# Reordering VectorE, ScalarE and GpSimd work at the passage between two transformer layers and inside the last attention pair

## The chip, the cores and the metric

The kernel is one program on one core of a Trainium2 chip. The core has a matrix engine (TensorE, PE in the profile; its loads of the stationary operand are shown as PEld), three elementwise engines (VectorE or DVE, ScalarE or ACT, GpSimd or POOL) and a sync engine (SyncE or SP), which here issues nearly all DMAs. Each engine runs its own list of instructions in order; semaphores tie the lists together. The metric is the device time of one execution in microseconds (us), taken as the median of the runs.

## The reference

A graph network block over 1024 nodes with 512 features: a graph convolution, four transformer layers, a second graph convolution, and residuals. Cut to the layer loop, which is where the change lies:

```python
for i in range(L):                                     # L = 4
    a = _attn(_ln(h, ln2_w[i], ln2_b[i]), cond, Wq[i], Wk[i], Wv[i], Wo[i])
    h = h + a
    u = _ln(h, ln3_w[i], ln3_b[i]) @ geglu_w[i] + geglu_b[i]
    val, gate = jnp.split(u, 2, axis=-1)
    f = val * jax.nn.gelu(gate, approximate=False)
    h = h + f @ ffo_w[i] + ffo_b[i]
```

`_attn` is cross attention: 16 batches of 64 queries, 256 conditioning rows each, 8 heads of 64. All is float32.

## The kernel before

The residual stream `h` stays on chip as eight blocks of 128 nodes by 512 features (`hall`; `h[nb]` is one block). A layer has an attention part, which runs over eight groups g (each a block of 128 query rows with its two batches of conditioning rows), and a feed-forward part in four stretches r.

Large products are done in fewer multiplications: a product of 2 x 2 blocks is computed as seven block products of sums and differences of blocks. The sums have to be made beforehand by DVE or POOL: `weight_sums` for the query weights (tiles `wqs`, four POOL instructions), `sum_first` for the normalised rows (`ln2S`), `geglu_weights` for the feed-forward weights (`ges`), `ln3_sums` (`ln3S`). Key and value products (`Twelve`) are instead done in three terms of reduced width: `right_parts` and `left_parts` split an operand x into a high part (`bh`, `ah`, by ACT), a low part (`bl`, `al`, by DVE) and a third (`bs` by DVE, `as` by POOL). Such a product has a `begin` (two terms, then ACT scales the PSUM bank in place, L373) and an `end` (third term, then a copy out by ACT, L380, or by DVE, L378). `staggered` runs a list of them so that the end of one follows the beginning of the next, and calls the functions of `beside` behind chosen ones.

PSUM has eight banks, handed out in turn; a new tile waits until the last reader of the bank's old tile is done. `pin` keeps an instruction in program order; `in_order(engine)` ties all instructions of one engine inside the block into the order in which they are written; `waiting_for(ins, engine)` makes the engine's instructions inside wait for `ins`; `issue_after(ins)` places instructions behind `ins` on their engine. What is not tied is placed by a scheduler.

**Inside the attention (g = 6).** `scores` makes the softmax, `keys` and `values` the products for the next group, and `mix` the weighting by the probabilities: it transposes the probabilities on PE (`tr_pr`), copies them out (`pT`, two by ACT, two by DVE at L880), multiplies (`po`, L866) and copies the result (`oT`, L889). At g = 6, after `mix`, `ln3_norm(4, 5)` normalises two blocks of `h`: statistics (L168, L169), a reciprocal root by a dozen small DVE operations (`rsqrt`, L151 to L160), and a scaling (`xn`, L189). Their transposes (`ln3_turn`, `tr_ln`) come after the transposes of blocks 0 to 3 and the last value product. At the same g POOL makes the four `ges` sums.

**The passage from layer l to l + 1.** The last output half of the feed-forward, `ffn_out(l, R - 1, 1, ...)`, adds seven products out of the banks `fa` to `fd` onto `h` (L1229, L1233, L1243). Its argument `beside` holds functions for other DVE work that is placed at fixed points: the roots of the first four blocks (`ready_first`), and, right behind the first product, `split_cond` (`al_c`, L314) and the moments of the first half of the blocks (`take_moments`). Behind it come the split of the value weights (`bl_wv`, `bs_wv`), the moments and roots of the second half (`less_ln`, L1344). DVE is tied in order through all this. Then the new layer starts: keys and values of group 0 by `staggered`, and beside them the scaling of the rows by ACT (`scaled_by_act`, four `xn` each, L1350) and their transposes (`turn_first`, `tr_ln`), taken out of PSUM by ACT (L810) and DVE (L808) in turn into `ln2T`. ACT is tied in order. `sum_first` makes the row sums of blocks 0 and 4, 1 and 5 on POOL and of the others on DVE (L231 to L234), and the queries (`QueryQuad`, products `qa` to `qd`) follow.

Of the kernel before, what the change touches and what calls it, by code (L numbers as in the profile page):

```python
# [14 lines left out]
OP = mybir.AluOpType  # L15
# [5 lines left out]
TINY = 2.0 ** -12  # L21
# [4 lines left out]
def gnn_kernel(  # L26
# [26 lines left out]
    nc = tc.nc  # L53
# [247 lines left out]
    def twelve_bits(t):  # L301
        return t.bitcast(F32R)
# [17 lines left out]
    def right_parts(x, name, room=None):  # L320

        parts = [slots_of(len(x), f"{n}_{name}") for n in ("bh", "bl", "bs")]
        for i, (h, l, s, x) in enumerate(zip(*parts, x)):
            nc.scalar.mul(twelve_bits(h), x, INWARD / TINY)
            for k in range(2):
                hk, lk, sk = (t[:, k, :] for t in (h, l, s))
                nc.vector.scalar_tensor_tensor(twelve_bits(l)[:, k, :], x[:, k, :], 1.0 / TINY, hk,
                                               OP.mult, OP.subtract)
                if room:
                    more = room(f"{name}_{i}_{k}")  # L330
                    nc.scalar.mul(more, hk, TINY)
                    nc.gpsimd.tensor_tensor(twelve_bits(s)[:, k, :], lk, more, OP.subtract)
                else:
                    nc.vector.scalar_tensor_tensor(twelve_bits(s)[:, k, :], hk, -TINY, lk,
                                                   OP.mult, OP.add)
        return parts

    def split_cond(l, g):
# [64 lines left out]
    def keys(l, g, wk, n=0, by=(0, 1)):  # L403

        to = blocks_in(kTs, g, f"kT_{l}_{g}")
        return [Twelve(f"k_{l}_{g}_{c}", wk, c, conds[g], to(c), by[c % 2]) for c in range(n, KC)]
# [127 lines left out]
    for i in range(2):  # L534
        for k in range(KC):
            hk = h0T[i][k // 2][:, k % 2, :]
# [316 lines left out]
    def mix(l, g, probs, v, hooks, each=pin):  # L853

        oT = t512(f"oT_{l}_{g}")
        po = bank(f"po_{l}_{g}")

        def weigh(c2, pTs):
            for a in range(2):
                c = 2 * c2 + a  # L860
                for b in range(2):
                    for m in range(MB):
                        for j in range(2):
                            n0 = c * P + b * NPG
                            at = (a * MB + m) * P + b * NPG
                            each(nc.tensor.matmul(  # L866
                                po[j * DH:(j + 1) * DH, n0:n0 + NPG],
                                v[b][:, m, c * P + j * DH:c * P + (j + 1) * DH],
                                pTs[j][:, at:at + NPG],
                                start=(m == 0), stop=(m == MB - 1)))  # L870

        turned = []
        for c2 in range(2):
            pTs = []
            for j in range(2):
                u = 2 * c2 + j
                pt = transposed(probs[u], f"pr_{l}_{g}_{u}", each)
                pT = t512(f"pT_{l}_{g}_{u}")
                if j:
                    nc.vector.tensor_copy(pT, pt)  # L880
                else:
                    nc.scalar.copy(pT, pt)
                pTs.append(pT)
            turned.append(pTs)
            hooks[c2]()
        weigh(0, turned[0])
        hooks[2]()
        weigh(1, turned[1])
        nc.vector.tensor_copy(oT, po)  # L889
        return oT  # L890

    def attn_out(l, g, oT, wo):
# [317 lines left out]
    def ffn_out(l, r, s, left, right, kept, each=lambda ins: ins, beside=()):  # L1210

        n = f"{l}_{r}_{s}"
        u = kept[s]
        a, b, c, d = (bank(f"{x}_{n}") for x in ("fa", "fb", "fc", "fd"))
        h11, h12, h21, h22 = (hall[:, 4 * i + 2 * s:4 * i + 2 * s + 2, j * M:(j + 1) * M]
                              for i in range(2) for j in range(2))

        def product(i, to, start):  # L1220
            for q in range(2):
                for k in range(2):
                    each(nc.tensor.matmul(to[:, q * M:(q + 1) * M],  # L1223
                                          left[i][k][:, (2 * s + q) * P:(2 * s + q + 1) * P],
                                          right[i][:, k, :], start=start and q == 0 and k == 0,
                                          stop=q == 1 and k == 1, skip_group_check=True))

        def add(to, of):
            each(nc.vector.tensor_tensor(to, halves_of(of), to, OP.add))  # L1229

        product(0, a, True)
        if r:
            each(nc.vector.tensor_tensor(u, a, u, OP.add))  # L1233
            for do in beside[2:]:
                do()
        else:
            nc.scalar.copy(u, a)
        product(6, c, True)
        add(h22, c)
        product(4, d, True)  # L1240
        add(h22, d)
        product(5, b, True)
        each(nc.vector.tensor_tensor(u, b, u, OP.add))  # L1243
        if r == R - 1:
            for to in (h22, h21, h12):
                add(to, u)
        for do in beside[:1]:
            do()
        product(1, a, False)
        add(h11, a)  # L1250
        for do in beside[1:2]:
            do()
        product(3, c, False)
        add(h21, c)
        product(2, d, False)
        add(h12, d)
# [83 lines left out]
    def scaled_by_act(blocks, mv, root, name):  # L1340

        n = len(blocks)
        less = small.tile([P, 4], F32, tag="less", name=f"less_{name}", bufs=2)[:, :n]
        scaled_by_act.last = nc.vector.scalar_tensor_tensor(less, mv.rearrange("p (n c) -> p n c", c=2)[:, :, 0], -1.0,  # L1344
                                       root, OP.mult, OP.mult)

        def scale():
            for i, nb in enumerate(blocks):
                xns[nb] = t512(f"xn_{name}_{nb}")
                nc.scalar.activation(xns[nb], h[nb], AF.Identity, bias=less[:, i:i + 1],  # L1350
                                     scale=root[:, i:i + 1])

        return scale
# [54 lines left out]
    for l in range(L):  # L1408

        lnS = []  # L1410
        if l:
            units = keys(l, 0, wk, by=(0, 0)) + values(l, 0, wv, by=(0, 0))
            to_turn = [0, 1, 4, 5], [2, 3, 6, 7]
        else:
            scale_first(1, deviations(mv_first[1], "ln2_0_4"))
            with waiting_for(scale_first.last, mybir.EngineType.Pool):
                wq = weight_sums(wq, "wqs_0")
            kTs[0], vs[0], kTs[1] = (begun[n] for n in ("k0", "v0", "k1"))
            units = keys(0, 0, wk, 2) + values(0, 0, wv, 1)
            to_turn = [0, 1, 2, 3], [4, 5, 6, 7]  # L1420

        def turn_some():
            nonlocal lnT, wq
            if l:
                lnT = [slots_of(2, f"ln2T_{l}_{i}") for i in range(2)]
            turn_first(l, to_turn[0])
            lnS.extend(ln_sums(l))
            if l:
                sum_first(nc.gpsimd, 0)
                sum_first(nc.gpsimd, 1)  # L1430
                with waiting_for(scaled_by_act.last, mybir.EngineType.Pool):
                    wq = weight_sums(wq, f"wqs_{l}")

        beside = {len(units) - 1: lambda: turn_first(l, to_turn[1])}
        if l:
            beside.update({1: to_scale.pop(0), 4: turn_some, 5: to_scale.pop(0)})
            with in_order(mybir.EngineType.Activation):
                staggered(units, beside)
        else:
            staggered(units, {2: turn_some, **beside})  # L1440
# [74 lines left out]
        for g in range(NG - 1):  # L1515
# [20 lines left out]
            v = values(l, g + 1, wv)  # L1536
            oTs.append(mix(l, g, probs, vs.pop(g), (k[-1].end, nothing, v[0].begin)))
            if g == NG - 2:
                ln3_norm(g - 2, g - 1)
            if g in (1, 2):  # L1540
                base_of(2 * l + g - 1)
            if l == 0:
# [182 lines left out]
        else:  # L1725
# [6 lines left out]
                for part, t in zip(wk, right_parts(raw_wk[i:i + 1], f"wk_{l + 1}_{i}")):  # L1732
                    part.extend(t)

            def condition_and_moments():
                split_cond(l + 1, 0)
                take_moments(l + 1, half[0])

            half = [0, 1, 4, 5], [2, 3, 6, 7]
            with in_order(mybir.EngineType.DVE):  # L1740
                ffn_out(l, R - 1, 0, fT, wff, kept, pin, (lambda: split_wk(0), lambda: split_wk(1)))
                ffn_out(l, R - 1, 1, fT, wff, kept, pin, (lambda: ready_first(l + 1, half[0]),
                                                          lambda: None, condition_and_moments))
                wq = load_w(Wq[l + 1], f"wq_{l + 1}")
                ffb = load_row(ffo_b, (l + 1) * D, f"ffb_{l + 1}")
                load_cond(l + 1, 1)
                wv = right_parts(raw_wv, f"wv_{l + 1}")
                take_moments(l + 1, half[1])
                ready_first(l + 1, half[1])
# [144 lines left out]
```

## Time and profile before

| what | us |
|---|---|
| median of the runs | 2437.28 |
| lowest and highest of three runs | 2433.90, 2438.86 |
| the profiled execution | 2432.47 |
| its span, first to last instruction | 2430.6 |
| DMA busy, mean of 16 engines, main queue | 16.6% |

The profile's page comes from one execution. Busy times are sums over instructions; PE's is of pipelined matmuls, so a busy PE is not a PE at its peak. A row of a timeline has the start in us from the beginning of the span, the length, the engine, the line of the kernel, the operation, `output<-input` with shapes, the number of equal instructions merged in the row, and in brackets the idle time of the engine before it with what ended that. A row of the view of waits has who waited for whom, and then total us, times and longest. A row of the view by windows has the stretch, its length, the busy time and count of instructions of PE, PEld, DVE, ACT and POOL, then the clock granted to PE (1 is full), the share of the DMA engines, and GB/s.

### The profile page before, as it was taken

How to read it: one execution, taken by the hardware profiler on the slowest of the kernel's cores; microseconds unless marked ns; L12 is line 12 of the kernel's file. 1: busy time of each engine (PE TensorE's matmuls, PEld its weight loads, DVE VectorE, ACT ScalarE, POOL GpSimd, SP SyncE). 2: the span in 40 equal slices, each digit the busy share in tenths (PEclk: the TensorE clock that was granted, in tenths of full speed). 3: DMA queues.
4: the chain of work that ended last, by engine and by line, in shares of the span. 5: the costliest groups of instructions: out<-in, count | busy, mean ns of one | idle time of the engine just before them, and what ended most of it. 6: DMA issues, size and time to landing. Idle time of an engine off the chain costs nothing. (4 is left out here: it accounts for less than half of the span.)

```text
span 2430.6 us, 33690 instructions
## 1 busy us (share of the span) xinstructions
PE 2367.9 (97%) x12528; PEld 1776.1 (73%) x12528; DVE 1596.9 (66%) x3016; ACT 999.5 (41%) x2023; POOL 940.0 (39%) x839
## 2 busy tenths in 40 slices
PE   8999999999989999999999999999999999999999
PEld 5668886677757887577776887477775888567787
DVE  9875456787764456877775455777785445678764
ACT  7444454343344444343343444433334444434320
POOL 0142233565233223565432223455514223356531
PEclk9999999999999999999999999999999999999999
DMA  6142110111301110021201101021121111011140
GB/s 199 31 140 83 57 66 18 47 41 53 109 31 61 40 49 23 22 65 44 104 15 64 66 19 53 9 61 44 44 91 53 44 53 35 18 52 35 53 148 36
DMA packets 108843, 138.31 MB, mean 57 GB/s; under 512 B 8232, under 2 KB 65904, under 8 KB 108672
## 3 DMA queue, kind: packets, MB, share of 16 engines
q1 hardware_dynamic: 106576, 130.64, 16.6%
q0 software_dynamic: 1376, 4.30, 0.5%
q8 instruction: 104, 1.70, 0.3%
q10 hardware_dynamic: 720, 1.11, 0.1%
q14 instruction: 67, 0.55, 0.1%
HBM read 119.25 MB, written 16.78 MB: 56 GB/s over the span
## 5 line engine op out<-in xcount | busy, mean ns | idle before, releaser
L316 POOL TENSOR_TENSOR as_c<-ah_c,al_c 128x512 fp32r<-128x512 f32 x128 | 189.6, 1511 | 191.8 <-DVE al_c L314 185.8
L1122 ACT ACTIVATE g<-g 128x512 f32<-128x512 f32 x192 | 112.1, 584 | 280.0 <-PE g L1108 277.5
L373 ACT ACTIVATE v<-v 128x512 f32<-128x512 f32 x127 | 74.0, 582 | 235.0 <-PE v L362 232.8
L1059 POOL TENSOR_TENSOR gsa<-gha,gla 128x512 fp32r<-128x512 f32 x96 | 125.8, 1331 | 103.8 <-DVE gla L1056 103.8
L1059 POOL TENSOR_TENSOR gsb<-ghb,glb 128x512 fp32r<-128x512 f32 x48 | 70.1, 1460 | 219.0 <-DVE glb L1056 219.0
L362 PE MATMUL v<-bh_wv,ah_c 128*128 128x512 f32 x508 | 148.3, 414 | 0.0
L362 PE MATMUL v<-bs_wv,as_c 128*128 128x512 f32 x508 | 144.1, 405 | 2.6 <-ACT v L373 2.4
L843 ACT ACTIVATE pr<-sc,nmax 128x256 f32<-128x256 f32 x256 | 118.1, 474 | 58.4 <-DVE nmax L838 58.4
L373 ACT ACTIVATE k<-k 128x512 f32<-128x512 f32 x125 | 72.6, 585 | 164.5 <-PE k L362 164.1
L362 PE MATMUL v<-bl_wv,al_c 128*128 128x512 f32 x508 | 137.0, 392 | 0.0
L1108 PE MATMUL g<-gr,gsa 128*128 128x512 f32 x384 | 136.4, 436 | 0.0
L1135 ACT ACTIVATE g<-g,gcols 128x512 f32<-128x512 f32 x96 | 67.5, 703 | 164.8 <-DVE g L1143 161.7
L362 PE MATMUL k<-ah_c,bh_wk 128*128 128x512 f32 x500 | 135.1, 392 | 0.0
L362 PE MATMUL k<-al_c,bl_wk 128*128 128x512 f32 x500 | 134.0, 390 | 0.0
L362 PE MATMUL k<-as_c,bs_wk 128*128 128x512 f32 x500 | 132.2, 395 | 0.0
L915 POOL TENSOR_TENSOR os<-oT 128x256 f32<-128x256 f32 x12 | 8.8, 734 | 318.8 <-DVE oT L889 318.8
L1223 PE MATMUL fa<-wff,fT 128*128 128x256 f32 x512 | 121.9, 381 | 6.7 <-DVE kept L1233 6.7
L1108 PE MATMUL g<-gr,gha 128*128 128x512 f32 x384 | 122.9, 401 | 0.0
L1108 PE MATMUL g<-gl,gla 128*128 128x512 f32 x384 | 119.0, 391 | 0.0
L1223 PEld LDWEIGHTS fa<-wff,fT 128*128 128x128 f32 x512 | 96.5, 190 | 26.7 <-DVE kept L1233 9.9
L362 PEld LDWEIGHTS v<-bs_wv,as_c 128*128 128x128 f32 x508 | 93.4, 188 | 28.9 <-ACT v L373 5.2
L314 DVE SCALAR_TENSOR_TENSOR al_c<-ah_c,ct 128x1024 fp32r<-128x1024 f32 x64 | 92.2, 1445 | 33.0 <-ACT ah_c L313 33.0
(368 smaller groups left out, 5891.2 us busy)
## 6 DMA issues: line engine op xcount, KB each, us to landing
ct<-cond_dram SPq DMA_DIRECT2D x48, 512.0 KB, 4.2
wff<-in_L_gnn_ffo_w_dram SPq DMA_DIRECT2D x32, 512.0 KB, 4.3
gxb<-in_L_gnn_geglu_w_dram SPq DMA_DIRECT2D x96, 128.0 KB, 2.2
gxa<-in_L_gnn_geglu_w_dram SPq DMA_DIRECT2D x96, 128.0 KB, 2.2
cond<-in_L_gnn_cond_dram SPq DMA_DIRECT2D x32, 256.0 KB, 3.5
cond_dram<-ct SPq DMA_DIRECT2D x16, 512.0 KB, 4.1
wk<-in_L_gnn_Wk_dram SPq DMA_DIRECT2D x8, 512.0 KB, 6.3
wv<-in_L_gnn_Wv_dram SPq DMA_DIRECT2D x8, 512.0 KB, 8.4
```

The source lines that it names most:

```text
L314: nc.vector.scalar_tensor_tensor(twelve_bits(l), h, -1.0 / TINY, x, OP.mult, OP.add)
L316: nc.gpsimd.tensor_tensor(twelve_bits(s)[:, k, :], h[:, k, :], l[:, k, :], OP.subtract)
L362: pin(nc.tensor.matmul(self.bank, twelve_bits(left[k // 2])[:, k % 2, self.c * P:(self.c + 1) * P], twelve_bits(right[k // 2])[:, k % 2, : ...
L373: nc.scalar.mul(self.bank, self.bank, 1.0 + TINY)
L843: nc.scalar.activation(pr3[:, a, :], ps3[:, a, :], AF.Exp, bias=nmax[:, a:a + 1], accum_out=tot[:, a:a + 1])
L915: t.tensor_tensor(s1, a21, a22, OP.add)
L1059: pin(nc.gpsimd.tensor_tensor(s_at, h_at, l_at, OP.subtract))
L1108: pin(nc.tensor.matmul(to, self.part(i, which)[:, k, :], self.rights[i][which].bitcast(F32R)[:, k, :], start=start and k == 0, stop=stop a ...
L1122: pin(nc.scalar.mul(to, to, 1.0 + TINY))
L1135: pin(nc.scalar.activation(to, of, AF.Gelu, bias=gcols[:, cg:cg + 1]))
L1223: each(nc.tensor.matmul(to[:, q * M:(q + 1) * M], left[i][k][:, (2 * s + q) * P:(2 * s + q + 1) * P], right[i][:, k, :], start=start and q ...
```

## The change

Four edits, all of order; no instruction is added or taken away.

1. In the passage: `ffn_out` calls only `beside[2]` (the split of the conditioning rows) behind its first product, and the rest (now the moments, a function of their own) after the adds of `fc` and `fd`.
2. In the passage: the query weights' sums are made ahead of the row sums on POOL, and wait for the last instruction of the value weights' split (`right_parts.last`) instead of that of the row scaling's preparation (`scaled_by_act.last`). The key tiles are allocated ahead of them.
3. In the passage: the four row scalings by ACT are called two at a time, one product apart.
4. In every layer, g = 6: `ln3_norm(4, 5)` is placed behind the copy `oT` of `mix`.

On PE and SyncE the order of instructions is the same before and after.

```diff
@@ right_parts
-                    nc.vector.scalar_tensor_tensor(twelve_bits(s)[:, k, :], hk, -TINY, lk,
-                                                   OP.mult, OP.add)
+                    right_parts.last = nc.vector.scalar_tensor_tensor(
+                        twelve_bits(s)[:, k, :], hk, -TINY, lk, OP.mult, OP.add)
@@ mix
-        nc.vector.tensor_copy(oT, po)
+        mix.last = nc.vector.tensor_copy(oT, po)
@@ ffn_out
         if r:
             each(nc.vector.tensor_tensor(u, a, u, OP.add))
-            for do in beside[2:]:
+            for do in beside[2:3]:
                 do()
...
         add(h22, d)
+        for do in beside[3:]:
+            do()
         product(5, b, True)
@@ scaled_by_act
-        def scale():
-            for i, nb in enumerate(blocks):
+        def scale(*which):
+            for i in which or range(n):
+                nb = blocks[i]
@@ the start of a layer
             units = keys(l, 0, wk, by=(0, 0)) + values(l, 0, wv, by=(0, 0))
+            units[0].to()
+            with waiting_for(right_parts.last, mybir.EngineType.Pool):
+                wq = weight_sums(wq, f"wqs_{l}")
...
                 sum_first(nc.gpsimd, 0)
                 sum_first(nc.gpsimd, 1)
-                with waiting_for(scaled_by_act.last, mybir.EngineType.Pool):
-                    wq = weight_sums(wq, f"wqs_{l}")
...
-            beside.update({1: to_scale.pop(0), 4: turn_some, 5: to_scale.pop(0)})
+            first, then = to_scale
+            to_scale.clear()
+            beside.update({1: lambda: first(0, 1), 2: lambda: first(2, 3), 4: turn_some,
+                           5: lambda: then(0, 1), 6: lambda: then(2, 3)})
@@ attention
             if g == NG - 2:
-                ln3_norm(g - 2, g - 1)
+                ln3_norm(g - 2, g - 1, behind=mix.last)
@@ the end of a layer
-            def condition_and_moments():
-                split_cond(l + 1, 0)
-                take_moments(l + 1, half[0])
...
                 ffn_out(l, R - 1, 1, fT, wff, kept, pin, (lambda: ready_first(l + 1, half[0]),
-                                                          lambda: None, condition_and_moments))
+                                                          lambda: None,
+                                                          lambda: split_cond(l + 1, 0),
+                                                          lambda: take_moments(l + 1, half[0])))
```

2 lines of the change are left out of this document (1 added, 1 removed).

## The prediction

> **What bounds the kernel now.** I read the page first, then what TensorE (PE) waited for, then the granted clock behind each wait, then the timelines of the two stretches that the change touches. The page's first part:
>
> ```profile
> PE 2367.9 (97%) x12528; PEld 1776.1 (73%) x12528; DVE 1596.9 (66%) x3016; ACT 999.5 (41%) x2023; POOL 940.0 (39%) x839
> ```
>
> PE is busy 97% of the span, and the change adds and removes no matmul, so it can only touch PE's idle time and the clock. The view of waits, PE alone (total, times, longest):
>
> ```profile
> PE po L866 <- DVE pT L880: 12.4, 4, 3.1
> PE qb L296 <- DVE ln2S L233: 8.1, 3, 2.7
> PE fc L1223 <- DVE hall L1229: 7.9, 3, 2.7
> ...
> PE v L362 <- ACT v L373: 2.4, 3, 0.8
> ```
>
> Four `po` waits lie in the attention of each layer at group g=6; the other three kinds come once in each of the three passages from one layer to the next. Together 30.8 us. The view by windows shows what they cost besides: each row is a stretch right behind such a wait, and the number after the POOL column is the clock granted to PE.
>
> ```profile
> 672.60:676.10 3.50, 3.46 (x9) 2.81 (x10) 3.34 (x7) 0.00 (x0) 1.01 (x1) 0.53 0.00 0
> 1847.10:1850.50 3.40, 3.40 (x5) 1.61 (x6) 0.31 (x1) 0.00 (x0) 0.00 (x0) 0.56 0.74 213
> 373.80:377.80 4.00, 4.00 (x68) 3.31 (x70) 1.12 (x2) 0.58 (x1) 0.00 (x0) 1.00 0.00 0
> 938.40:942.40 4.00, 3.97 (x36) 3.43 (x37) 1.16 (x2) 0.00 (x0) 0.00 (x0) 0.57 0.00 0
> 1504.50:1508.80 4.30, 4.29 (x37) 3.60 (x38) 1.15 (x2) 0.00 (x0) 0.00 (x0) 0.60 0.00 0
> 2072.00:2076.00 4.00, 3.88 (x36) 3.44 (x37) 1.26 (x3) 0.00 (x0) 0.00 (x0) 0.58 0.01 4
> ```
>
> Rows 1 and 2 follow an `fc` and the third `qb`, rows 3 to 6 the four `po`. Except in layer 0 the clock is near half for a few us after a `po` wait of 3.1 us. A stretch at clock c and length t loses (1-c) x t: 0.43 x 4.0 = 1.7, 0.40 x 4.3 = 1.7, 0.42 x 4.0 = 1.7 behind the last three `po`, 0.47 x 3.5 = 1.65 behind `fc`, 0.44 x 3.4 = 1.5 behind the third `qb`.
>
> **Part 1: norms tied behind the weighting (once in each of four layers).** Timelines of VectorE (DVE), GpSimd (POOL) and PE at g=6 of layer 1:
>
> ```profile
> 926.31 1.27 DVE L168 BATCH_NORM_STATS2 st_ln<-hall 128x6 f32<-128x512 f32 x2
> 927.83 1.11 DVE L151 TENSOR_SCALAR v_ln<-mv_ln 128x2 f32<-128x2 f32 x1
> 929.18 2.24 DVE L156 SCALAR_TENSOR_TENSOR a_ln<-y_ln,v_ln 128x2 f32<-128x2 f32 x1
> 933.98 2.21 DVE L156 SCALAR_TENSOR_TENSOR a_ln<-y_ln,v_ln 128x2 f32<-128x2 f32 x1
> 937.69 0.68 DVE L880 COPY pT<-tr_pr 128x512 f32<-128x512 f32 x1
> 944.27 0.69 DVE L889 COPY oT<-po 128x512 f32<-128x512 f32 x1 [4.71 <-PE po L866]
> 944.88 0.99 DVE L189 TENSOR_SCALAR xn_ln<-hall,mv_ln,y_ln 128x512 f32<-128x512 f32 x2
> 949.93 0.69 DVE L378 COPY v<-v 128x512 f32<-128x512 f32 x1 [4.05 <-PE v L362]
> ...
> 928.99 2.41 POOL L239 TENSOR_TENSOR wgate<-wval,wgate 128x1024 f32<-128x1024 f32 x1
> 933.81 2.36 POOL L241 TENSOR_TENSOR ges<-wval,ges 128x1024 f32<-128x1024 f32 x1
> 955.89 1.42 POOL L231 TENSOR_TENSOR ln3S<-ln3T,ln3T 128x256 f32<-128x256 f32 x2 [19.71 <-DVE ln3T L808]
> ...
> 934.02 1.04 PE L201 MATMUL tr_pr<-ident,pr 128*128 128x128 f32 x8
> 938.43 1.77 PE L866 MATMUL po<-pT,v 128*64 128x64 f32 x30 [3.11 <-DVE pT L880]
> 954.22 1.04 PE L201 MATMUL tr_ln<-ident,xn_ln 128*128 128x128 f32 x8
> ```
>
> The reciprocal root of the norms is a dozen operations on 128x2 numbers, and here single ones of them last 1.1 to 2.2 us. Each long one ends where a POOL sum ends: the one from 929.18 at 931.42, POOL's L239 at 931.40; the one from 933.98 at 936.19, POOL's L241 at 936.17. So DVE is held by POOL's weight sums; the copies kT and pT stand behind it in DVE's order, and PE waits for pT. In the changed order all of the norm but the two scalings, which were there already, comes after the copy oT. The transposes end by about 935.1 and a pT copy takes 0.68, so PE has no wait: 4 x 3.1 = 12.4, and 3 x 1.7 = 5.1 of clock, 17.5 in all.
>
> Is it paid back? oT moves from 944.27 to about 939.5 (3.1 + 1.7 earlier). Behind it come statistics (926.31 to 927.83: 1.5), the root without POOL's hold (2.4, next fence), scalings 1.0: done near 945.0. POOL's sums are over at 936.17 and its next work starts at 955.89, or 4.8 earlier. PE wants the result at 954.22 - 4.8 = 949.4, so 4.4 us are spare. Queued behind the norm on DVE is the copy of v, then due at 949.93 - 4.8 = 945.1: in time. Without that cover this part would cost what rival C says. Bounds: 12.4 (the clock is halved elsewhere instead) to 17.5; I take 17.5.
>
> The Trainium skill, "TensorE: Matmul & The Clock Gate", Part 1, has the clock drop after at least one idle window of about 3.4 us and asks for no gap above that. By it no `po` wait would cost clock, and this part would be 12.4. The rows show the drop behind waits of 3.1 and of 2.7 us, though not behind every one, so they decide.
>
> **Part 2: the passage between layers (three times).** DVE, then ACT, POOL and PE of the first one:
>
> ```profile
> 666.46 2.35 DVE L314 SCALAR_TENSOR_TENSOR al_c<-ah_c,ct 128x1024 fp32r<-128x1024 f32 x2
> 671.92 0.66 DVE L1229 TENSOR_TENSOR hall<-fc,hall 128x512 f32<-128x512 f32 x1
> 684.56 0.69 DVE L334 SCALAR_TENSOR_TENSOR bs_wv<-bh_wv,bl_wv 128x512 fp32r<-128x512 f32 x1
> 688.49 0.17 DVE L151 TENSOR_SCALAR v_ln<-mv 128x4 f32<-128x4 f32 x1
> 690.74 0.16 DVE L1344 SCALAR_TENSOR_TENSOR less_ln<-mv,y_ln 128x4 f32<-128x4 f32 x1
> 691.70 0.41 DVE L808 TENSOR_SCALAR ln2T<-tr_ln,cols 128x128 f32<-128x128 f32 x1 [0.80 <-ACT ln2T L810]
> 710.50 1.49 DVE L233 TENSOR_TENSOR ln2S<-ln2T,ln2S 128x256 f32<-128x256 f32 x1
> 714.11 0.41 DVE L233 TENSOR_TENSOR ln2S<-ln2T,ln2S 128x256 f32<-128x256 f32 x1
> ...
> 696.42 0.59 ACT L373 ACTIVATE v<-v 128x512 f32<-128x512 f32 x1
> 702.12 0.58 ACT L380 COPY v<-v 128x512 f32<-128x512 f32 x1 [0.29 <-PE v L362]
> 702.60 0.47 ACT L810 ACTIVATE ln2T<-tr_ln,cols 128x128 f32<-128x128 f32 x1
> ...
> L238 POOL TENSOR_TENSOR wqs<-wq,wq x4: 1299/1302/1306, 127.8 to 1831.0; 128x512 f32<-128x512 f32 x4
> 706.64 6.47 POOL L316 TENSOR_TENSOR as_c<-ah_c,al_c 128x512 fp32r<-128x512 f32 x4
> ...
> 697.06 1.19 PE L362 MATMUL v<-bs_wv,as_c 128*128 128x512 f32 x4
> 714.67 1.95 PE L296 MATMUL qb<-ln2S,wqs 128*128 128x512 f32 x4 [2.69 <-DVE ln2S L233]
> ```
>
> *Sums ahead of moments.* The adds that free the banks of fc and fd follow al_c directly, at 668.8 instead of 671.92. PE's 2.65 wait and 1.65 of clock go, and PE comes to the key products 4.3 us sooner. But DVE's sum of work up to less_ln (690.90) is the same, and it has next to no idle time to give (3.34 busy of the 3.50 in the first windows row). The transposes of the normalised rows are taken out by ACT (L810) and DVE (L808) in turn, DVE's share standing behind less_ln, and ACT's scaling of v at 696.42 stands behind that chain. PE's product at 697.06 needs this scaling, which ended at 697.01: that chain sets this place already. PE's 4.3 us turn into a wait there. Gain here: at most 691.70 - 690.90 = 0.8, and only if DVE is no later than now.
>
> *Weight sums ahead of row sums.* Four POOL sums of 1.30 now start when bs_wv is done (685.25) and last until 690.45, over the root that starts at 688.49. By the hold seen in part 1, v_ln waits for the third sum (689.15), a_ln for the fourth (690.45); nine operations at 0.2 follow, to 692.4. The chain then starts at about 692.45, 0.75 later than now. Bounds: 0.8 earlier (no hold) to 1.1 later. I take 0.75 later, since g=6 shows just these operations held. The wait at 697.06 becomes about 4.3 + 0.75 = 5 us, and half clock behind it is likely. That costs up to 1.7 of PE time, but PE's next work here is again paced by ACT, which has four row scalings to do; I put 0 to 0.5 of it on the path.
>
> *Scaling in smaller pieces.* The scalings of v no longer stand behind four row scalings; PE's 0.8 goes, but ACT's work up to 702.60 is the same except for the 0.29 it waited for PE: -0.3. The second chain starts about 0.45 late (0.75 - 0.3; 1.1 early to 1.3 late).
>
> *Second chain, 702.60 to 714.67.* DVE alone takes 0.41 for a row sum but 1.49 while POOL runs as_c. Weight sums leave POOL here, so as_c starts sooner and covers less of the row sums. Half of the eight can be slowed, by at most 1.49 - 0.41 = 1.1 each: a gain of 4.4 at most, but as_c with its 6.5 us still covers half the chain. Against it, ACT now makes two copies of the query partials, each waiting for PE, ahead of an L810 that DVE needs: at most one slowed sum's worth, +1.1. Bounds -4.4 to +1.1; I take -0.5, near the middle of what a shifted cover gives. So `qb` starts where it does now, from 5.5 earlier to 2.9 later (0.5 of half clock in it). Whether half clock follows `qb` (once in three now) I put at even odds: -0.5 over the three.
>
> **Sum.** Against the profiled execution, 2432.47 with a span of 2430.6: -17.5 - 0.5 = -18, which gives 2414.5. That execution lies 4.8 below the median of the runs, so the median goes from 2437.28 to about 2419.
>
> **Rivals.**
>
> A. *The passages gain what their waits show:* 7.9 + 8.1 + 2.4 + clock 3 x 1.65 + 1.5 = 24.9 more, or about 2395; half of it 2407. For it: PE would really start 4.3 earlier. Against it: DVE without a gap to 690.90. Chance 0.13.
>
> B. *The passages lose:* `qb` late by 2.9, and half clock behind each: 3 x (2.9 + 1.5) = 13, or 2437.3 - 17.5 + 13 = 2433. For it: POOL over the root, a longer wait at v. Chance 0.13.
>
> C. *Slower:* the moved norm is itself held, as before, by POOL. It then needs some 9 us for the root (from 927.83; the second copy behind it starts at 937.69) instead of 2.4, and is done near 952: 2.5 too late for tr_ln and 6.7 too late for the copy of v and the take-outs behind it. PE waits between these two, say 4.5, plus 1.7 of clock: 4 x 6.2 = 25 against the 17.5 gained, or +7: 2444. It decides from 4.4 us of lateness on; POOL's gap from 936.17 speaks against it. Chance 0.03.
>
> D. *The wait at `po` only moves:* the transposes or another bank hold PE at the same place, part 1 brings a third: 2431. Against it: the same mixes with g other than 6 have no such wait (four in all). Chance 0.05.
>
> **Numbers.** My forecast has 0.66, with 2411 to 2427 as its own range. Leaving out the full form of A, the far end of B, and C, eight times in ten gives 2408 to 2429. A difference below 0.2% (4.9 us) is what this measurement cannot tell from none. Faster by more: 0.66 + 0.13 + most of B and D, 0.93. Same: 0.04. Slower: 0.03.
>
> **What would show it.** PE's list of waits without `po` behind pT; roots at g=6 at 0.2 us an operation; no half clock behind `po`. In the passages no wait at fc, instead about 5 us before the v product behind ACT's scaling, long operations in the second root while POOL sums the query weights, `qb` within 3 us of its place. The forecast is wrong if v's product is reached without a wait (A), or if PE waits for tr_ln or the copy of v at g=6 (C).

## The result and the profile after

The kernel after took 2414.39 us in the median of four runs (2413.25 to 2417.47), beside 2437.97 for the kernel before on the same chip (2433.90 to 2438.86): a ratio of 0.9909, 95% interval 0.9891 to 0.9926. The profiled execution took 2414.67 with a span of 2412.9, against 2432.47 and 2430.6 before: 17.7 us less, where the prediction's sum had 18. The page's first part:

```profile
PE 2360.7 (98%) x12528; PEld 1773.0 (73%) x12528; DVE 1571.4 (65%) x3016; ACT 1000.1 (41%) x2023; POOL 937.1 (39%) x839
```

DVE is 25.5 us less busy with the same 3016 instructions (1596.9 before), though no work was taken away: some of its instructions must be shorter. The view of waits, PE alone (who waited for whom: total us, times, longest):

```profile
PE v L362 <- ACT v L373: 15.6, 3, 5.2
PE fa L1223 <- DVE kept L1233: 6.7, 8, 0.8
...
PE qb L296 <- DVE ln2S L233: 5.4, 3, 1.8
```

The waits for `po` (12.4) and for `fc` (7.9) are gone. `qb` went from 8.1 to 5.4, and the wait before the `v` product from 2.4 to 15.6. So of the waits' 30.8 us 21.0 are left. The view by windows at the places that matter (the number after the POOL column is the clock granted to PE):

```profile
692.90:699.80 6.90, 5.88 (x14) 4.63 (x15) 0.41 (x1) 5.58 (x10) 4.67 (x7) 0.51 0.00 0
932.40:936.40 4.00, 4.00 (x69) 3.29 (x70) 0.69 (x1) 0.86 (x2) 1.20 (x1) 1.00 0.00 0
712.20:715.80 3.60, 3.51 (x9) 1.63 (x10) 1.09 (x2) 0.00 (x0) 0.00 (x0) 1.00 0.74 263
1255.90:1260.00 4.10, 3.67 (x9) 2.93 (x10) 0.34 (x1) 4.10 (x8) 4.02 (x6) 0.58 0.00 0
1815.90:1822.90 7.00, 5.36 (x13) 4.19 (x14) 1.02 (x3) 5.44 (x10) 5.01 (x8) 0.51 0.00 0
```

Row 2 is the weighting at g=6 in layer 1: full clock, where row 4 of the prediction's windows had 0.57. Row 3 is the first `qb`: full. The other three lie behind the three waits for `v`, at half clock, two of them for 7 us.

Group g=6 of layer 1, POOL, DVE and PE of the timeline:

```profile
928.78 2.38 POOL L240 TENSOR_TENSOR ges<-ges,wval 128x1024 f32<-128x1024 f32 x1
931.24 2.37 POOL L241 TENSOR_TENSOR ges<-wval,ges 128x1024 f32<-128x1024 f32 x1
...
932.53 0.69 DVE L880 COPY pT<-tr_pr 128x512 f32<-128x512 f32 x1 [0.18 <-PE tr_pr L201]
936.75 0.69 DVE L889 COPY oT<-po 128x512 f32<-128x512 f32 x1 [3.53 <-PE po L866]
939.29 0.16 DVE L156 SCALAR_TENSOR_TENSOR a_ln<-y_ln,v_ln 128x2 f32<-128x2 f32 x1
941.06 1.00 DVE L189 TENSOR_SCALAR xn_ln<-hall,mv_ln,y_ln 128x512 f32<-128x512 f32 x2
942.41 0.69 DVE L378 COPY v<-v 128x512 f32<-128x512 f32 x1 [0.35 <-PE v L362]
...
932.42 1.15 PE L866 MATMUL po<-pT,v 128*64 128x64 f32 x32
946.70 1.03 PE L201 MATMUL tr_ln<-ident,xn_ln 128*128 128x128 f32 x8
```

`po` has no bracket: PE came to it without a wait. The root runs at 0.16 an operation behind `oT`, POOL's sums being over at 933.61. The normalised rows are done at 942.06 and PE wants them at 946.70, so 4.6 us are spare (the prediction said 4.4), and DVE had even idled 0.35 for PE before its copy of `v`.

The first passage, DVE, POOL, ACT and PE:

```profile
662.71 2.35 DVE L314 SCALAR_TENSOR_TENSOR al_c<-ah_c,ct 128x1024 fp32r<-128x1024 f32 x2
664.98 0.68 DVE L1229 TENSOR_TENSOR hall<-fc,hall 128x512 f32<-128x512 f32 x1
684.76 0.81 DVE L151 TENSOR_SCALAR v_ln<-mv 128x4 f32<-128x4 f32 x1
685.81 1.13 DVE L156 SCALAR_TENSOR_TENSOR a_ln<-y_ln,v_ln 128x4 f32<-128x4 f32 x1
688.54 0.16 DVE L1346 SCALAR_TENSOR_TENSOR less_ln<-mv,y_ln 128x4 f32<-128x4 f32 x1
708.99 1.49 DVE L233 TENSOR_TENSOR ln2S<-ln2T,ln2S 128x256 f32<-128x256 f32 x1
711.73 0.41 DVE L233 TENSOR_TENSOR ln2S<-ln2T,ln2S 128x256 f32<-128x256 f32 x1
...
684.25 1.29 POOL L240 TENSOR_TENSOR wqs<-wqs,wq 128x512 f32<-128x512 f32 x1
685.62 1.30 POOL L241 TENSOR_TENSOR wqs<-wq,wqs 128x512 f32<-128x512 f32 x1
703.85 6.34 POOL L316 TENSOR_TENSOR as_c<-ah_c,al_c 128x512 fp32r<-128x512 f32 x4 [6.21 <-DVE al_c L314]
...
693.27 0.59 ACT L373 ACTIVATE v<-v 128x512 f32<-128x512 f32 x1
699.50 0.58 ACT L373 ACTIVATE v<-v 128x512 f32<-128x512 f32 x1 [1.30 <-PE v L362]
700.62 0.58 ACT L380 COPY v<-v 128x512 f32<-128x512 f32 x1 [0.54 <-PE v L362]
...
693.91 2.07 PE L362 MATMUL v<-bs_wv,as_c 128*128 128x512 f32 x4 [5.20 <-ACT v L373]
712.29 1.96 PE L296 MATMUL qb<-ln2S,wqs 128*128 128x512 f32 x4 [1.80 <-DVE ln2S L233]
```

The add of `fc` now follows `al_c` directly. In the second root one operation ends at 685.57 and one at 686.94, where POOL's L240 and L241 end at 685.54 and 686.92: the hold of g=6, at a smaller size. PE then waits 5.20 for ACT's scaling of `v`. Behind that the half clock shows on another engine too: the `v` product takes 2.07 where before it took 1.19, and ACT, which had waited 0.29 for PE at L380 before, waits 1.30 and 0.54.

Where the 17.7 us came from can be read by cutting both spans at two rows of each passage, the start of `al_c` and the second group of `qb` (8.66 behind the first where the clock is full), as the timelines have them:

| stretch | before | after | difference |
|---|---|---|---|
| start to the first `al_c` | 666.46 | 662.71 | -3.75 |
| passage 1 | 56.87 | 58.24 | +1.37 |
| between 1 and 2 | 509.29 | 504.16 | -5.13 |
| passage 2 | 56.99 | 57.06 | +0.07 |
| between 2 and 3 | 509.15 | 504.14 | -5.01 |
| passage 3 | 58.46 | 57.98 | -0.48 |
| from there to the end | 573.38 | 568.61 | -4.77 |

The four stretches with a g=6 in them gave 18.7, and the three passages together cost 1.0.

### The profile page after: what moved, and what is told of

Its sections match the earlier page's. It is cut to its first block, busy times and chain, and to the rows that moved or that the text cites. A ratio compares the mean times of both kernels' runs of the same rounds, so it can differ in the third digit from the quotient of the medians.

```text
span 2412.9 us, 33707 instructions
## 1 busy us (share of the span) xinstructions
PE 2360.7 (98%) x12528; PEld 1773.0 (73%) x12528; DVE 1571.4 (65%) x3016; ACT 1000.1 (41%) x2023; POOL 937.1 (39%) x839
## 5 line engine op out<-in xcount | busy, mean ns | idle before, releaser
L362 PE MATMUL v<-bs_wv,as_c 128*128 128x512 f32 x508 | 146.8, 411 | 15.6 <-ACT v L373 15.6
L378 DVE COPY kT<-k 128x512 f32<-128x512 f32 x54 | 37.4, 692 | 118.3 <-PE k L362 110.1
```

Of the source, the lines that this page charges most:

```text
L362: pin(nc.tensor.matmul(self.bank, twelve_bits(left[k // 2])[:, k % 2, self.c * P:(self.c + 1) * P], twelve_bits(right[k // 2])[:, k % 2, : ...
L378: nc.vector.tensor_copy(self.to(), self.bank)
```

## The experiments

Each row of times is the median of its kernel, with the ratio to the kernel before on the same chip; the row of the kernel before has the range of its medians on the chips of the experiments. All diffs are against the kernel after unless it is said otherwise. The waits of "ACT takes the first half" are those of a second run of that kernel, which took 2404.62 (0.9873, 0.9853 to 0.9893).

| kernel | us | ratio, 95% interval | PE waits: `po`, `fc`, `v`, `qb` |
|---|---|---|---|
| before | 2434.55 to 2438.46 | 1 | 12.4, 7.9, 2.4, 8.1 |
| after | 2414.39 | 0.9909, 0.9891 to 0.9926 | 0, 0, 15.6, 5.4 |
| norms alone | 2416.49 | 0.9922, 0.9905 to 0.994 | 0, 8.0, 3.2, 8.1 |
| passage alone | 2434.51 | 1.0, 0.9991 to 1.001 | 12.4, 0, 15.7, 5.4 |
| before, POOL's sums later | 2414.25 | 0.9913, 0.9896 to 0.993 | 0, 8.0, 2.4, 8.0 |
| after, weight sums back | 2414.69 | 0.9916, 0.9899 to 0.9932 | 0, 0, 11.0, 6.4 |
| after, adds back | 2412.75 | 0.9898, 0.988 to 0.9916 | 0, 8.0, 3.8, 5.4 |
| ACT takes the first half | 2403.45 | 0.9857, 0.984 to 0.9875 | 0, 0, 5.7, 5.4 |
| that, and weight sums later | 2408.06 | 0.9877, 0.9859 to 0.9895 | 0, 0, 1.4, 11.4 |
| that, and the split later | 2390.70 | 0.9808, 0.9791 to 0.9826 | 0, 0, 1.4, 0 |
| after, the split later | 2408.80 | 0.989, 0.9873 to 0.9906 | 0, 0, 15.8, 0 |
| ACT takes, the split later | 2395.91 | 0.9837, 0.9821 to 0.9854 | 0, 0, 5.6, 0 |
| the best, adds back | 2400.42 | 0.9854, 0.9838 to 0.9871 | 0, 8.0, 1.4, 0 |

**Which part pays.** Two kernels split the change: the kernel before with edit 4 alone, and the kernel after without it (edits 1 to 3).

```diff
-        nc.vector.tensor_copy(oT, po)
+        mix.last = nc.vector.tensor_copy(oT, po)
...
-                ln3_norm(g - 2, g - 1)
+                ln3_norm(g - 2, g - 1, behind=mix.last)
```

> The kernel before with the fourth edit alone (norms behind the weighting). Theory: all four waits of po behind pT go (12.4 us) and with them three stretches of half clock (5.1), so 17.5 us less than before, a span near 2413; the passages keep their waits at fc (2.65 each), at v (0.8) and at qb (2.7). Rival: the passages brought a good part of the 23.6 us between the medians; then the norms alone bring 12 or less.

> The changed kernel with the fourth edit undone (the three edits of the passage alone). Theory: PE's 4.3 us per passage turn up again as a wait of about 5 us before the product of v behind ACT's scaling, and qb starts 0 to 2 us later than before, counted from al_c; the time is that of before, from 2 us less to 6 more. Rival: the passages gain, 6 us or more less than before.

Edit 4 alone brings 18.1 us by the medians (2434.55 to 2416.49), and its `po` waits are gone while `qb` and `fc` stay as they were. Edits 1 to 3 alone bring 0.0, within 0.1% either way, and trade `fc` for `v` as in the kernel after. Within the intervals the two parts add up to the whole change (0.9922 and 1.0 beside 0.9909). By the medians 5.5 us of the 23.6 are missing, of which 3.4 lie in the kernel before, whose median was 2437.97 there and 2434.55 here.

**Is it POOL?** The norms could be late because they stood ahead of the copies, or because POOL held them there. In the kernel before, only POOL's four `ges` sums are moved, behind `oT`; DVE's order stays, with the whole norm ahead of the copies `pT`.

```diff
+        mix.last = nc.vector.tensor_copy(oT, po)
...
-            if g == NG - 2:
-                with waiting_for(scores.last, mybir.EngineType.Pool):
-                    left = geglu_weights(l, 0, *raw)
...
+                with waiting_for(mix.last, mybir.EngineType.Pool):
+                    left = geglu_weights(l, 0, *raw)
```

> The kernel before with POOL's four ges sums at g = 6 made to wait for the copy oT; the norm stays where it was, ahead of the copies kT and pT on DVE, and no engine's order changes. Theory (the hold by POOL is what made the norm long): every operation of that root takes 0.2 us, the copies are on time, no po wait, about 17 us less than before. Rival (the place in the queue is what costs): the root's dozen operations and the statistics still delay pT, and at least 2 of the 3.1 us stay.

Its timeline at g=6 of layer 1, DVE, PE and POOL:

```profile
926.49 0.16 DVE L156 SCALAR_TENSOR_TENSOR a_ln<-y_ln,v_ln 128x2 f32<-128x2 f32 x1
928.06 0.16 DVE L160 SCALAR_TENSOR_TENSOR y_ln<-b_ln,y_ln 128x2 f32<-128x2 f32 x1
933.35 0.69 DVE L880 COPY pT<-tr_pr 128x512 f32<-128x512 f32 x1 [0.18 <-PE tr_pr L201]
...
933.24 1.15 PE L866 MATMUL po<-pT,v 128*64 128x64 f32 x32
...
938.33 2.62 POOL L238 TENSOR_TENSOR ges<-wgate,wgate 128x1024 f32<-128x1024 f32 x1 [15.03 <-DVE oT L889]
```

With POOL silent the same dozen operations in the same place take 0.16 each, the copies are in time and `po` has no wait. It took 2414.25: as much gain as edit 4 (20.3 us against 18.1, with overlapping intervals). So DVE's queue was no obstacle; the overlap with POOL was. That is the mechanism of part 1, and the Trainium skill states it, "SBUF — State Buffer", section "Who interferes with whom": a DVE instruction with two inputs in SBUF contends with a GpSimd instruction that reads SBUF, one in a mode with two ports contends with GpSimd too, and the shared pair of ports is an exclusive lock, in the second case held by whichever issues first for its whole instruction. The traces agree, down to the time at which a held operation ends, and they show it for operations on two numbers a partition.

**Does POOL over the second root cost anything?** Edit 2 undone:

```diff
-            units[0].to()
-            with waiting_for(right_parts.last, mybir.EngineType.Pool):
-                wq = weight_sums(wq, f"wqs_{l}")
...
+                with waiting_for(scaled_by_act.last, mybir.EngineType.Pool):
+                    wq = weight_sums(wq, f"wqs_{l}")
```

> The changed kernel with the query weights' sums put back behind the row sums on POOL. Theory (POOL holds DVE's small operations): no operation of the second root in the passage lasts over 0.2 us, the first take-out of the turned rows comes about 0.7 us earlier counted from al_c, the wait before the product of v falls from 5.2 to about 4.5; the sums then lie in the second chain again and lengthen it by up to 1. In total within 3 us of the changed kernel. Rival: the sums have no part in it, the wait stays at 5.2.

No operation of the root is over 0.17 now, the wait at `v` falls from 5.2 to 3.7 and that of `qb` rises from 1.8 to 2.3 at most; the time is that of the kernel after (2414.69 against 2414.39). So the hold costs the chain to `v` about 1.5 us: DVE's first take-out comes 24.33 behind `al_c` without it, 25.91 with it and 25.24 in the kernel before. That is 0.9 earlier without a hold, where the prediction had at most 0.8, and 0.7 later with it, where it took 0.75. The 1.5 does not reach the total because of the clock. Without edit 2, `qb` starts 0.4 to 1.6 sooner (41.31 to 41.34 behind the first key product, against 41.77 to 42.94), but waits longer, and half clock follows it in all three passages, where in the kernel after it followed in none: its second group comes 10.32 to 10.36 behind the first instead of 8.66. The view by windows behind the first `qb`:

```profile
710.00:716.00 6.00, 5.09 (x8) 2.27 (x9) 1.88 (x5) 0.00 (x0) 0.00 (x0) 0.72 0.54 175
```

**Is the first edit worth anything?** Edit 1 undone:

```diff
-            for do in beside[2:3]:
+            for do in beside[2:]:
                 do()
...
-        for do in beside[3:]:
-            do()
```

> The changed kernel with the first edit undone (moments ahead of the adds of fc and fd again). Theory (VectorE's work, not PE, sets when the product of v can end): the wait at fc of 2.65 us is back in each passage, the wait before the product of v shrinks by the same and the half clock, to 1 to 2.5 us, and the time is within 3 us of the changed kernel. Rival (the edit saves its 2.65 us and clock): 8 to 13 us more than the changed kernel.

The 8.0 us at `fc` are back, those at `v` fall from 15.6 to 3.8, and the time is not above that of the kernel after (2412.75 against 2414.39, intervals of the ratios overlap). PE's earlier start is all lost at the next wait, as the prediction's first step has it. In the traces the three passages are even 0.7 to 1.9 us shorter with the edit undone (56.31, 56.34 and 57.19), because half clock follows `v` in one of them only, for 3.4 us.

**What holds `v`.** ACT's scaling stands behind the take-outs of the transposed rows, which ACT and DVE share in turn, so ACT waits for DVE's root. If ACT takes out the whole first half alone, its part gets longer but no longer waits for `less_ln`:

```diff
-    def turn_first(l, blocks):
+    def turn_first(l, blocks, by=(0, 1)):
...
-            turn(xn, lnT[nb // 4], c0, LN2W + l * KC, LN2B + l * KC, f"ln2_{l}_{nb}", each=pin)
+            turn(xn, lnT[nb // 4], c0, LN2W + l * KC, LN2B + l * KC, f"ln2_{l}_{nb}", by, each=pin)
...
-            turn_first(l, to_turn[0])
+            turn_first(l, to_turn[0], (0, 0) if l else (0, 1))
```

> The changed kernel, but ACT alone takes the first half of the turned rows out of PSUM (sixteen pieces, no share of VectorE). Theory (the take-outs stand behind VectorE's second moments and root, and ACT's scaling of v behind the take-outs): sixteen pieces at about 0.36 us take ACT some 6 us from the first transpose on, so v is scaled about 4 us earlier counted from al_c; the wait of 5.2 falls to 1 or so, without half clock, and the passage ends 4 to 6 us earlier, 12 to 18 us less than the changed kernel in all. Rival (PE's wait only moves on to qb, which stands behind other work of VectorE): qb's wait grows by as much and the time stays within 3 us.

2403.45, some 11 us less than the kernel after, a little under the 12 to 18 expected. The chain of norms was what set `v`. With it goes the half clock: the view by cores has a clock of 0.999 in the trace of the second run, 0.996 in the kernel after. What is short of the expectation is that same hold again: with the rows taken out sooner, POOL's row sums fall on the second root, `less_ln` ends 28.8 behind `al_c` instead of 26.0, ACT waits 1.9 for it, and some 1.9 us a passage of the wait at `v` are left.

**A miss: the weight sums behind the root.** To free the root as well, the weights' sums were made to wait for it:

```diff
-            with waiting_for(right_parts.last, mybir.EngineType.Pool):
+            with waiting_for(scaled_by_act.last, mybir.EngineType.Pool):
```

> As the run before, and the query weights' sums wait for the second root instead of the split of the value weights. Theory: the root is free of POOL's hold (no operation over 0.2 us, root 1.5 us shorter), but with ACT taking out the rows alone nothing on the path waits for it any more, so the time is that of the run before within 2 us. Rival: the hold still costs 1.5 us in each passage, 4 us less than the run before.

It took 2408.06, 4.6 more. Neither theory had that. Timeline of the first passage, POOL, DVE and PE, and then the view by windows behind `qb`:

```profile
696.51 1.59 POOL L232 TENSOR_TENSOR ln2T<-ln2T,ln2T 128x256 f32<-128x256 f32 x1
698.06 1.81 POOL L233 TENSOR_TENSOR ln2S<-ln2T,ln2S 128x256 f32<-128x256 f32 x1
700.64 5.48 POOL L316 TENSOR_TENSOR as_c<-ah_c,al_c 128x512 fp32r<-128x512 f32 x4
...
703.52 1.48 DVE L233 TENSOR_TENSOR ln2S<-ln2T,ln2S 128x256 f32<-128x256 f32 x1
704.92 1.48 DVE L231 TENSOR_TENSOR ln2S<-ln2T,ln2T 128x256 f32<-128x256 f32 x1
...
707.87 2.66 PE L296 MATMUL qb<-ln2S,wqs 128*128 128x512 f32 x4 [3.89 <-DVE ln2S L233]
```

```profile
707.80:712.00 4.20, 4.13 (x6) 1.69 (x7) 1.07 (x2) 0.00 (x0) 0.00 (x0) 0.64 0.70 242
```

POOL's row sums of the first half come late and fall on DVE's `al_c`, which slows them from 0.73 to 1.59 and 1.81; `as_c` starts later; three of DVE's row sums take 1.44 to 1.48 and a fourth 1.00, where 0.41 is their own time. PE, no longer held at `v`, waits 3.89 for them, and half clock follows. To see which of the two costs the time, the kernel without this edit was run once more and its trace read:

> The kernel after, with ACT alone taking out the first half of the turned rows, once more, for its trace. Taking the query weights' sums behind the second root (the run with both) should have saved 0 to 4 us and cost 4.6. Theory: in this kernel POOL sums the weights over the root and then the first half's rows, and is done with both before 694 in the first passage, against 700.7 with both; so as_c starts right behind al_c and covers one or two of DVE's row sums (1.4 us or more each), where with both four are slowed. The waits of qb come to 5 to 8 us over three, against 11.4 with both. Rival: the waits of qb are the same within 1 us, and the difference is half clock. Time 2403 in either case.

POOL's last row sum starts there 22.92 behind the first key product of the passage, against 30.38; one DVE sum is slowed fully (1.49) and one to 0.73; the waits of `qb` come to 5.4. So far the theory. But counted from the first key product `qb` starts at 38.19, 38.21 and 38.55 in the three passages, and with the sums moved at 38.30, 38.29 and 38.25: no later. The second group of `qb` comes at 46.85 to 47.21 in the one and at 48.60 to 48.65 in the other. What the edit costs, 1.4 to 1.8 us a passage or 5.0 in all, lies behind `qb`: PE gets there sooner, waits 2 us longer, and pays it in half clock. The rival had the cost right, with unequal waits.

**What holds `qb`.** DVE makes `al_c` for the second condition in the midst of the row sums, and POOL's `as_c` behind it slows them. Both are needed only by the next group. They were put behind the row sums:

```diff
-        sum_first(nc.vector, 3)
-        split_cond(l, 1)
+        rows_summed = sum_first(nc.vector, 3)
+        with tc.issue_after(rows_summed.ins) if l else nullcontext():
+            split_cond(l, 1)
```

It was run in three settings: with both of the edits above, with neither, and with ACT's take-outs only.

> As the run before, and the split of the next conditioning rows (ah_c, al_c, as_c of group 1) stands behind the row sums instead of inside the second chain. Theory: VectorE's 3 us of al_c leave the chain and POOL no longer holds its row sums (1.49 to 0.41), so qb starts some 3 us earlier, its wait goes, and the time is 5 to 9 us below the run before. Rival: the split is now late for the keys of group 1 and PE waits there for as_c instead; no gain.

> The kernel after, with only the split of the second condition (al_c, as_c) put behind the second half's row sums, as in the best run so far. Theory: DVE's row sums run at 0.4 each, qb is reached without a wait, and the first product of queries without DVE's split beside it ends a little sooner: 5.4 + 0.7 = 6 less than after, 2408.5; the wait at v with its half clock stays (15.6). Rival 1: the gain needs ACT alone at the first half too, and this brings less than 2: 2413 or more. Rival 2: as_c, now some 4 us later, is late for the next group's products, a new wait there, slower than after by some us.

> The kernel after with ACT alone at the first half's rows and the split of the second condition behind the row sums; the query weights' sums stay over the second root, as after has them. Theory: with qb out of the way nothing waits for POOL's row sums or for the root (less_ln 1.5 later, but ACT is busy with the first half until 688.9), so the waits are those of the run with the sums moved as well (no v wait over 0.5, no qb wait) and the time is the same within 2: 2389 to 2393. Rival 1: the 4.6 by which moving the sums cost come back here: 2386. Rival 2: the held root delays the second half's scalings and with it v: 1 to 1.5 a passage, 2394 or more.

With both it took 2390.70, 17.4 less than without the split moved, where 5 to 9 were expected. The timeline of its first passage, DVE and PE:

```profile
687.31 0.16 DVE L1346 SCALAR_TENSOR_TENSOR less_ln<-mv,y_ln 128x4 f32<-128x4 f32 x1
700.14 0.42 DVE L233 TENSOR_TENSOR ln2S<-ln2T,ln2S 128x256 f32<-128x256 f32 x1
702.72 2.35 DVE L314 SCALAR_TENSOR_TENSOR al_c<-ah_c,ct 128x1024 fp32r<-128x1024 f32 x2
...
696.92 7.13 PE L296 MATMUL qa<-ln2T,wq 128*128 128x512 f32 x16 [0.74 <-ACT ln2T L810]
703.90 1.88 PE L296 MATMUL qb<-ln2S,wqs 128*128 128x512 f32 x4
```

Row sums take 0.42 (the first of them 0.51), `qb` follows `qa` without a gap, the rival's wait at the keys of group 1 does not show, and the clock is 1.00 over the whole span. From the first key product to the second group of `qb` it is 42.74 to 42.78 where it was 48.60 to 48.65: 5.9 a passage, 4.1 of them ahead of `qb` and 1.8 of half clock behind it. The expectation had counted the wait and left out the clock. In the kernel after alone the split brings 5.6 by the medians (2408.80) and 6.2 in the three passages of the traces, as its theory had, and `v` keeps its 15.8. With ACT's take-outs but the weight sums over the root it took 2395.91, 5.2 more than the best (4.9 between the profiled spans): its rival 2. Timeline of the first passage of that kernel, DVE, POOL, ACT and PE:

```profile
691.02 0.59 DVE L1346 SCALAR_TENSOR_TENSOR less_ln<-mv,y_ln 128x4 f32<-128x4 f32 x1
...
687.00 0.74 POOL L231 TENSOR_TENSOR ln2S<-ln2T,ln2T 128x256 f32<-128x256 f32 x1
...
691.65 1.52 ACT L1353 ACTIVATE xn_ln<-hall,less_ln,y_ln 128x512 f32<-128x512 f32 x2 [1.90 <-DVE less_ln L1346]
...
693.70 1.20 PE L362 MATMUL v<-bs_wv,as_c 128*128 128x512 f32 x4 [1.40 <-ACT v L373]
698.62 7.13 PE L296 MATMUL qa<-ln2T,wq 128*128 128x512 f32 x16 [1.05 <-ACT ln2T L810]
```

POOL's row sums now start at 687.00, right over the rest of the root, and hold it again (0.59 for an operation of 0.16). Counted from `al_c`, `less_ln` comes 4.0 later than in the best kernel; ACT waits 1.90 for it, and counted from the first key product `qa` starts 1.9 to 2.0 later, three times. So the place of the weight sums is worth +4.6 in one setting and -5.2 in the other.

**The first edit again.** If PE's earlier start was only lost at the next wait, it must count where that wait is gone. The best kernel with edit 1 undone, by the same diff as above:

> The best run so far (2390.7) with the first edit undone: the moments ahead of the adds that free the banks of fc and fd, as before. Alone, undoing this edit in the kernel after changed nothing (2412.75 against 2414.39). Theory: it changed nothing there because PE's 4 us only turned into the wait at v; in the best run this wait and that of qb are gone, so the wait of 2.7 at fc, now again in place, is paid in full, with half clock behind it: 3 x (2.7 + 0 to 1.7) = 8 to 13 more, 2399 to 2404. Rival: in the best run too the chain of norms sets the passage, and PE's 4 us are lost elsewhere: within 2 of 2390.7.

2400.42: 9.7 more than with edit 1, on another chip, where the kernel before had 2434.89 (2438.46 on that of the best); the ratios differ by 0.0046, or 11 us. The profiled spans differ by 8.4 (2397.4 against 2389.0). PE waits of that kernel:

```profile
PE fc L1223 <- DVE hall L1229: 8.0, 3, 2.7
```

The wait is paid in full. The clock stayed at 1.0 in the profiled execution and at 0.999 in the others, so the half clock counted in the expectation's upper end did not come.

## Why the prediction was right, point by point

*Part 1, 17.5.* Right. The stretches with a g=6 gave 18.7 in the profiled pair, edit 4 alone 18.1 by medians. The mechanism (POOL over the root) was shown by moving POOL alone. The cover of 4.4 us was 4.6, and neither `tr_ln` nor the copy of `v` waits. The term is 1.2 us short. With PE's rows of the two kernels laid side by side, the products come 3.4 to 3.5 us earlier from each `po` on, where the list of waits has 3.11, and the half clock behind three of them gives 1.4 to 1.5 more, where 1.7 was counted; another 0.3 of the first stretch is a wait ahead of the first layer (L349, 1.93 before and 1.63 after).

*Part 2, "Sums ahead of moments".* Right: PE came to the key products 4.5 to 4.6 us sooner (6.63 behind `al_c` instead of 11.13 to 11.24; 4.3 was said), and that became the wait at `v` (5.20 where "about 5" was said). The run with edit 1 undone, and the best kernel with it undone, show both halves of it: nothing in the kernel after, 8 to 11 us once the next waits are gone.

*"Weight sums ahead of row sums".* The place and the operations held were right, two of them, ending with L240 and L241, and so was the size: DVE's first take-out is 0.67 later behind `al_c` (0.75 was said). The half clock behind the wait is the term that was mis-sized: 0 to 0.5 on the path was said, because ACT paced what follows. But ACT's scalings of `v` need PE's products, and at half speed PE became the slower: ACT's waits of 1.30 and 0.54 are 1.8 us against 0.29 before. The half clock lasted 6.8 us in passages 1 and 3 and 3.4 in passage 2 (the record at the end). The run with edit 1 undone gives its price on the path: its first take-out stands in the same place (25.92 to 25.95 behind `al_c`), and in passages 1 and 2, where no half clock follows `v`, `qb` starts 47.65 and 47.67 behind `al_c`. In the kernel after it starts at 49.57, 48.40 and 49.31: 1.9, 0.7 and 1.7 later, or 0.7 to 1.0 for each 3.4 us at half clock.

*"Scaling in smaller pieces".* Edit 3 was not tried alone, so what it is worth stays open. The 0.8 that PE waited between two products is gone.

*"Second chain", -0.5.* A little better: in the first passage from the first L810 of the second half to `qb` 12.07 before, 11.19 after, or -0.9, though one row sum is still slowed fully (1.49). It starts 2.25 later (36.14 and 38.39 behind `al_c`), so that `qb` comes 1.4 later in passage 1, within the 3 us given.

*Clock behind `qb`, even odds.* None in the three passages after, once before: that is worth 1.5 in passage 3 (10.12 between the first two groups of `qb` before, 8.66 after), which is 0.5 shorter in all, while passage 1 is 1.4 longer. In sum the passages cost 1.0 where -0.5 was said, and part 1 brought 1.2 more. That the sum of 18 came so near to 17.7 is luck in part: the two errors nearly cancel.

*The rivals.* A fell: PE did start 4.5 earlier and `v` did wait. C and D fell: no wait at `tr_ln`, none at `po`. B had its mechanism in part (POOL over the root, half clock, though behind `v` and not behind `qb`); it had the passages lose 13, and they lost 1.0.

*The step to the median.* It was said that the profiled execution before lay 4.8 below its median, and that after would too. It did not: 2414.67 profiled, 2414.39 in the median. Hence 2414 and not 2419, and 23.6 between medians where the profiled pair shows 17.7. The clock that is listed with each run says where most of such a difference comes from: among the kernel before's runs beside the experiments, the five with a clock of 0.996 have spans of 2429.3 to 2429.9, and the five with 0.992 spans of 2436.2 to 2438.1. So its runs differ by how much half clock they met, and the profiled one (0.995, 2430.6) met little. The kernel after's four runs lie at 0.996 and 0.997. The change therefore takes more half clock out of a usual run than out of the profiled one, on which the sum was built.

## What to carry to other kernels

A wait's price is not its length in a list: removing it pays only if the next thing is not already late, so follow the chain to the next wait, and once that is gone try again the edits that brought nothing (the first edit: 0 in the kernel after, 8 to 11 us where the waits at `v` and `qb` are gone). Keep small operations of VectorE that stand on the path from running beside a long GpSimd sum: here ones of 0.16 took up to 2.3 beside sums of 2.4. Moving either engine helped, and every move should be followed to what it overlaps next. The version that came out best here keeps all four edits, lets ScalarE take out the first half alone, puts the weight sums behind the second root and the split of the second condition behind the row sums: 2390.70, ratio 0.9808.

## What the runs showed of the hardware that was not expected

The half clock comes in pieces on a fixed grid. The stretches of the span in which the trace's record of the clock has 0.5, start in us and length:

```
before  672.5 x 3.41   938.7 x 3.41  1239.1 x 3.41  1505.3 x 3.41  1805.7 x 3.41  1846.6 x 3.41  2071.9 x 3.41
after   693.0 x 6.83  1256.2 x 3.41  1816.0 x 6.83
```

Starts before differ by whole multiples of 3.413 (266.2 is 78 of them, 300.4 is 88, 41.0 is 12). In the kernel before, half clock followed where PE was idle for 2.3 us or more of one such piece (`fc`, the third `qb`, three of the `po`), and did not follow the same 3.1 us wait in layer 0, which the grid cut into 1.4 and 1.7. So whether a wait of about 3 us costs clock is a matter of phase. After waits of 5.2 it came each time, for one or two pieces. The Trainium skill, "TensorE: Matmul & The Clock Gate", Part 1, has this free-running window of 3413 ns; that a window idle for a part is enough is only in these traces. With PE's idle time summed over each piece of the grid in all kernels, the least that brought half clock from full is 1.90 (the kernel after with the weight sums back) and the most that did not is 1.91 (the passage alone): by PE's modelled ends the border lies a little over half of a piece.

The hold between VectorE and GpSimd goes both ways: beside `al_c` GpSimd's row sums took 1.59 and 1.81 instead of 0.73.
